# Filter samples loaded early, filter stores and first ffn loads by GpSimd, branch matrices one in two steps, the first image's lags kept for the tail

## The chip, the core and the metric

The kernel runs on one core of one Trainium2 chip, as a single launch. A core has a matrix engine (TensorE, PE in the profile, with its weight loads as PEld), VectorE (DVE), ScalarE (ACT), GpSimd (POOL) and SyncE (SP). Each engine works through its own queue in order. Transfers (DMA) are issued from the queues of SP, ACT and POOL, and an issue that waits for a semaphore holds up what stands behind it in its queue. The metric is the device time of the launch in microseconds (us), the median of several executions.

## What is computed

The input is two images of 128 channels and 64 x 64 places, all in 32-bit floats. Layer 0 is a neighbourhood-attention block. Layer 1 takes the 4096 places of an image as tokens: a full attention of normalised tokens with themselves, then a "spectral" ffn: causal convolutions with 16 filters, mixed by four branches' matrices, and three short lags. Cut to what matters:

```python
# layer 0: group norm, then a neighbourhood-attention block on NHWC tokens
x = x + _L0_conv_ref(_gn(x), ...)          # 7x7 neighbourhood attention, 4 heads, three 128x128 products
# layer 1 on tokens t of shape (2, 4096, 128)
t = t + _L1_attn_ref(_ln_t(t))             # all 4096 tokens, own key left out
t = t + _L1_ffn_ref(_ln_t(t), ...)
...
def _L1_attn_ref(q):
    sim = jnp.einsum('blh,bmh->blm', q, q) * scale
    sim = jnp.where(diag[None, :, :], jnp.float32(-1000000000.0), sim)
    attn = jax.nn.softmax(sim, axis=-1)
    return jnp.einsum('blm,bmh->blh', attn, q)
...
def _compute_spectral(u, sigma, phi, Mpp, Mpm):
    U_plus, U_minus = _stu_conv(phi, u, PADDED_SL)     # causal convolutions with 16 filters
    s = sigma ** SIGMA_POW
    out = jnp.einsum('btkd,k,kde->bte', U_plus, s, Mpp)
    return out + jnp.einsum('btkd,k,kde->bte', U_minus, s, Mpm)
def _compute_ar_u(Mu, u):                              # three short lags
    for i in range(Mu.shape[0]):
        ui = jnp.pad(u, ((0, 0), (i, 0), (0, 0)))[:, :sl]
        out = out + jnp.einsum('btd,de->bte', ui, Mu[i])
...
for i, frac in enumerate((1, 2, 4, 8)):                # four branches, on the first T / frac tokens
    si = _stu(x[:, :T // frac], sigma, phi, M_u[i], M_phi_plus[i], M_phi_minus[i])
...
weights = y_hard - jax.lax.stop_gradient(y_soft) + y_soft   # softmax of log_weights + gumbel
return jnp.sum(stacked * weights, axis=-1)
```

## The kernel before, in words

**Stages.** Layer 0 comes first (0 to about 344 us), written out as an explicit plan of pieces. Then follow the full attention of image 0 (`attention(0, fill)`, about 344 to 762 us), the attention of image 1 (`attention(1, fill)`, about 762 to 1187 us), a short tail, and the convolution of the ffn in a transformed domain (from about 1235 us to the end). The tail and the convolution work on both images.

**The attention** goes over 36 pairs of 512-token chunks, four steps each. A step multiplies keys with queries (L927, L936), ACT makes exponentials (L932, L943), and PE multiplies them with the values (L985 for the chunk's own sum, L1057 for the other chunk's). As the matrix of weights is symmetric, its transpose serves the other chunk too: ACT stores the exponentials of four steps to memory (`sent`, tile eb, L959), SP loads them back in another layout (`moved`, tile et, L966, four loads), DVE finishes the transposition in blocks (`turned`, L975), and PE uses them some steps later. MOVE, TURN and DELAY give the numbers of steps between these.

**The filler.** After each step, `fill()` runs one piece of other work. First it lets `stores()` send one queued store, or two where more than three are queued. Then it asks the generators in `urgent`, then those in `steps`: a plain `yield` ends the fill, `yield True` passes the turn on to the next queue. Within most of the attention the order of all engines is that of the program, so the filler decides what stands where in each queue.

**What the filler carries.** In image 0: `drain` (what is left of layer 0), `branch_weights` (loads lw, gu and sg by SP; its pow of sg stands on POOL at L1252; then loads of m_u), `filters`, and `tokens(1)`. In image 1: what is left of image 0's chains, its lags, `for_ffn`. Urgent are the chains `after(b, c)`, one for each finished chunk: transposes to tokens (L1123), statistics on DVE (L183, L184) with a pow on POOL (L174), normalisation (L191), transposes back (L202), products with the transform tr (L1175, L1189), copies by ACT (tile uo, L1156), sums and differences (tile ub, L1160, on POOL during attention, on DVE in the tail), and stores to us. The stores go through a list: `fresh` enters one, `room()` sends old ones until at most three buffers' worth is waiting, as the tag "ub" has four buffers.

**`filters`** loads the filter samples by SP in four parts (tile pn, L1344, two buffers shared with the branch matrices), turns their order round on DVE (L1361), transforms them on PE (L1382), and adds up running sums on ACT and DVE (L1389, L1391). For each of 12 steps POOL makes sum and difference (fb, L1395), and in eight of them also their negative (fn, L1407). The 32 stores of these to gs are issued from ACT's queue.

**`short_lags(b, h)`** first copies the residual back (four steps), then makes four groups of three products with mu (L1221), added on DVE (L1237). There are two such generators for each image, so eight groups. In image 0 the groups are put into `steps` of the second attention, except one that the filler runs at the end of the first.

**`for_ffn`** waits until a piece of the first image's memory (`spare`) has been used and given back, takes the first image's memory over, and loads inv and, through `filter_matrices`, 32 parts of the branch matrices by POOL (tile st, L1299). They are added up on DVE with the branches' weights (L1321, L1323) and scaled on ACT (L1334), three loads ahead. At the end `load_blocks` loads the first four blocks of the convolution, each with four ct loads and one ut load, from SP's queue (L1484, L1492).

**The tail** runs the last chains of image 1 two at a time, with lag groups of image 1 between them. The memory of chains and stores is used again by the convolution's y, so the convolution's first copies (L1599) wait for the last stores.

Of the kernel before, what the change touches and what calls it, by code (L numbers as in the profile page):

```python
# [14 lines left out]
P = 128  # L15
# [6 lines left out]
KF = 16  # L22
# [80 lines left out]
def kernel(  # L103
# [773 lines left out]
    with ap_:  # L877
# [21 lines left out]
        zc = [tp.tile([P, 2, TH + 1], F32, name="zc"), tt0.rearrange("p (s t) -> p s t", s=2)]  # L899
        nc.gpsimd.memset(zc[0][:, :, 0:1], 0.0)  # L900

        def attention(b, fill):
# [183 lines left out]

        spare = [tok[0][:, 0:4, :]]
        adder = [nc.gpsimd]
# [26 lines left out]
        def after(b, c):  # L1115
# [20 lines left out]
            yield  # L1136
            borrowed = b == 1 and spare not in ([], [None])
            z = spare.pop() if borrowed else sp.tile([P, 4, P], F32, tag="z4", name="z4")
            stats = ln_statistics(kept_)
            yield True  # L1140
            yield True
# [55 lines left out]

            if borrowed:
                spare.append(None)

# [101 lines left out]
        def filter_matrices(mpl, mmi, pool):  # L1302

            parts_ = [(k0, dst, src, i) for k0 in range(0, KF, 4) for dst, src in ((mpl, m_plus), (mmi, m_minus)) for i in range(NBR)]
            to_come = iter(enumerate(parts_))
            loaded = []

            def load():
                for at, (k0, _, src, i) in to_come:
                    loaded.append(branch(src[:, k0 : k0 + 4], i, pool if at % 4 > 1 else None))  # L1310
                    return

            for _ in range(3):
                load()
                yield
            for k0, dst, src, i in parts_:
                load()
                st = loaded.pop(0)
                dst2 = dst[:, k0 : k0 + 4].rearrange("p k e -> p (k e)")
                if i == 0:  # L1320
                    nc.vector.tensor_scalar(dst2, st, wt[:, 0:1], None, ALU.mult)  # L1321
                else:
                    nc.vector.scalar_tensor_tensor(dst2, st, wt[:, i : i + 1], dst2, ALU.mult, ALU.add)  # L1323
                yield
                if dst is mpl or i + 1 < NBR:
                    continue
                a, d = (m[:, k0 : k0 + 4, :].rearrange("p k e -> p (k e)") for m in (mpl, mmi))
                s = sp.tile([P, 512], F32, tag="uo", name="mdiff", bufs=2)
                nc.vector.tensor_tensor(s, a, d, ALU.subtract)
                nc.vector.tensor_tensor(a, a, d, ALU.add)  # L1330
                for k in range(4):
                    ks = slice(k * P, (k + 1) * P)
                    for to, of in ((a, a), (d, s)):
                        nc.scalar.activation(  # L1334
                            to[:, ks], of[:, ks], AF.Identity, bias=0.0, scale=sg[:, k0 + k : k0 + k + 1]
                        )
                yield

        def filters():

            def lags(hh, e):

                pn = sp.tile([P, KF, 2, LG], F32, tag="st", name="pn")
                nc.sync.dma_start(  # L1344
                    out=pn.rearrange("p k l f -> p (k l) f"),
                    in_=bass.AP(
                        phi_pad.tensor, P - FB + (2 * P * hh + e) * FB, [[2 * FB, P], [PHW, 2 * KF], [1, LG]]
                    ),
                )
                return pn  # L1350

            ph = {}
            for hh in range(SG // 2):
                pns = [lags(hh, e) for e in range(2)]
                for _ in range(3):
                    yield
                for e, pn in enumerate(pns):
                    at = (2 * hh + e) * LL
                    ph[hh, e] = cm[1][:, at : at + LL].rearrange("p (l f k) -> p l f k", l=2, f=LG)
                    for l in range(2):  # L1360
                        nc.vector.tensor_copy(ph[hh, e][:, l], pn[:, :, l, ::-1].rearrange("p k f -> p f k"))  # L1361
            yield

            def store(src, r0, n, ri, s, i, o):
# [3 lines left out]
                )  # L1368
                fresh(to, src, nc.scalar)

            everything = [(r0, c0 + ri * P, (ri,), P) for r0, c0 in row_tiles for ri in range(2)]
            everything.append((left_row, left_col, (0, 1), 64))
            for r0, c0, parts_, m in everything:
                places = cm[1][:, SG * LL : (3 * SG) * LL].rearrange("p (j e c) -> p j e c", j=SG, e=2)
                for j in range(SG):
# [27 lines left out]
                    if 1 in parts_:  # L1403
                        mine = slice(m - n, m)
                        room()
                        fn = sp.tile([P, 2, LL], F32, tag="ub", name="fn", bufs=4)
                        nc.gpsimd.tensor_scalar(fn[mine], fb[mine], -1.0, None, ALU.mult)  # L1407
                        store(fn[mine], r0, n, 1, s, 1, 0)
                    yield

        def residual_of(lags):
# [3 lines left out]

        def filler(b, steps, kept=None):

            urgent, done = [], []
            crowd_[0] = urgent

            def fill(c=None):
# [10 lines left out]

                stores()
                for queue in (urgent, steps):
                    while queue:
# [36 lines left out]

        def blocks(q):


            ct = ctp.tile([P, 2, 2 * (FB + 2) * KF], F32, tag="ct", name="ct")
            for o in range(2):
                for l in range(2):
# [4 lines left out]
                    at = l * (FB + 1) * KF  # L1483
                    nc.sync.dma_start(out=ct[:, o, at : at + (FB + l) * KF], in_=src)  # L1484
            return ct

        first_blocks = []

        def inputs(b, q):

            ut = utp.tile([P, 2, P], F32, tag="ut", name="ut")
            nc.sync.dma_start(  # L1492
                out=ut,
# [4 lines left out]
        def load_blocks():  # L1498
            for q in range(4):
                ct = blocks(q)  # L1500
                yield
                first_blocks.append((ct, inputs(0, q)))
                yield
# [5 lines left out]
        def for_ffn():  # L1509

            nonlocal mpl, mmi, inv, mu1, ctp, utp
            while spare != [None]:
                yield True
            first_.close()
# [4 lines left out]
            inv = l1.tile([P, K2 // BC * 4 + 1, CQ], F32, name="inv")  # L1519
            ctp = ctx.enter_context(tc.tile_pool(name="blocks", bufs=5))  # L1520
            nc.gpsimd.tensor_copy(mu1, mu)
            nc.gpsimd.dma_start(out=inv, in_=nc.inline_tensor(t_out, "t_out").ap().rearrange("(a p) c -> p a c", p=P))
            with tc.tile_pool(name="mix", bufs=2) as mixp:
                yield from filter_matrices(mpl, mmi, mixp)
            utp = ctx.enter_context(tc.tile_pool(name="inputs", bufs=4))

# [4 lines left out]

        steps = [*left, *kept, for_lags(), for_ffn()]


        kept = []
        fill, left = filler(1, steps, kept)
        attention(1, fill)
        adder[:] = [nc.vector]
        crowd_[0] = [None, None]
        for gen in steps:  # L1540
            for _ in gen:
                pass
        *chains, residuals = left
        while chains:
            for gen in chains[:2]:
                if next(gen, 0) == 0:
                    chains.remove(gen)
                stores()
            next(kept[0], None)
        stores_left()  # L1550
        for _ in residuals:
            next(kept[0], None)
        for _ in kept[0]:
            pass
# [330 lines left out]
```

## Time and profile before

| what | value |
|---|---|
| three executions, us | 2010.49, 2010.69, 2013.98 (median 2010.69) |
| the profiled execution, us | 2008.28 |
| its span, us | 2006.6 |
| mean granted clock of PE | 0.984 |
| busy, us: PE, DVE, ACT, POOL | 1912.1, 943.3, 733.1, 728.1 |
| the chain that ended last, by engine | PE 78%, DVE 8%, POOL 6%, DMA 4%, issue 2%, ACT 1% |
| DMA queue of SP (q1) | 221,874 packets, 26.2% of 16 engines' span |
| DMA queue of ACT (q10) | 13,758 packets, 8.2% |
| DMA queue of POOL (q0) | 18,848 packets, 5.7% |
| et loads by SP | 216 of 256 KB |
| us stores by POOL | 64 of 256 KB (3.1 us to landing), 128 of 32 KB (3.9 us) |
| gs stores by ACT | 12 of fb and 4 of fn of 256 KB, 12 and 4 of 64 KB |
| branch matrices by POOL | 32 of 256 KB (5.8 and 5.9 us to landing) |
| filter samples by SP | 4 of 128 KB |

The profile is of one execution. Its slices divide the span in 40 equal parts, and each digit is a busy share in tenths. Rows by stretch give the start and end, the length, then for each engine the busy time and the number of instructions, the clock that PE was granted, and the DMA engines' busy share. Rows in order of time give the start, the length, the engine, the line, the operation, the tiles and a count. A bracket at the end is the time that the engine had stood idle before, and the engine and line that ended it. An engine name with q (SPq, ACTq) is the issue of a transfer from that engine's queue. Times are us unless marked ns.

### The profile page before, as it was taken

What the parts mean: (1) busy time and instruction counts of PE and PEld (TensorE: products, weight loads), DVE (VectorE), ACT (ScalarE), POOL (GpSimd) and SP (SyncE); (2) the same over time, 40 slices, a digit from 0 to 9 for tenths busy, and PEclk for the clock granted to TensorE, in tenths of its full rate; (3) what the DMA queues carried; (4) which work ended last, traced back from release to release, by engine and by line L of the source; (5) the groups of instructions that cost most, each with busy time, mean ns of one, the idle gap of its engine ahead of it and who ended that gap; (6) DMA issues with size and microseconds to landing.
All of it is one profiled execution on the core that took longest, in us unless ns stands there. A gap on an engine that the chain in (4) does not pass through costs nothing.

```text
span 2006.6 us, 50785 instructions
## 1 busy us (share of the span) xinstructions
PE 1912.1 (95%) x20504; PEld 1353.1 (67%) x20504; DVE 943.3 (47%) x2918; ACT 733.1 (37%) x1718; POOL 728.1 (36%) x1183
## 2 busy tenths in 40 slices
PE   6899998999899999999999997999999999999998
PEld 4577776444344444444444444999999999999987
DVE  5799996453454434343654355333333343333332
ACT  3788986322133233212323223222222222222221
POOL 4467887314432345404333344222222212222211
PEclk8999999999999999999999998999999999999999
DMA  5222221568575643838787623222222223222211
GB/s 155 62 62 61 61 60 41 174 163 234 167 201 160 171 121 106 244 91 251 230 222 192 168 68 84 69 66 67 67 68 56 54 73 87 66 68 66 68 39 44
DMA packets 254713, 226.20 MB, mean 113 GB/s; under 512 B 130543, under 2 KB 210431, under 8 KB 247056
## 3 DMA queue, kind: packets, MB, share of 16 engines
q1 hardware_dynamic: 221874, 126.86, 26.2%
q10 hardware_dynamic: 13758, 63.28, 8.2%
q0 software_dynamic: 18848, 32.82, 5.7%
q8 instruction: 163, 2.67, 0.6%
q14 instruction: 70, 0.57, 0.1%
HBM read 131.40 MB, written 91.25 MB: 111 GB/s over the span
## 4 chain that ended last, share of the span: by engine, by line
PE 78%; DVE 8%; POOL 6%; DMA 4%; issue 2%; ACT 1%; SPq 0%; DVEq 0%; ACTq 0%; POOLq 0%
PE acc L1613 28%; PE own L985 11%; PE bank L927 7%; PE pc L1594 7%; PE other L1057 6%; PE bank L349 2%; PE bank L559 2%; PE bank L202 2%; PE bank L936 2%; PE bank L1175 1%; DVE et L975 1%; POOL us L1093 1%; PE bank L1221 1%; DMA us<-ub 1%; PE bank L523 1%
## 5 line engine op out<-in xcount | busy, mean ns | idle before, releaser
L1599 DVE COPY y<-pc 128x512 f32<-128x512 f32 x320 | 206.2, 686 | 347.1 <-PE pc L1594 345.9
L1613 PE MATMUL acc<-y,mpl 32*128 32x256 f32 x5120 | 323.7, 380 | 0.8 <-DVE af L1623 0.8
L1613 PE MATMUL acc<-y,mmi 32*128 32x256 f32 x5120 | 315.8, 375 | 0.0
L1599 ACT COPY y<-pc 128x512 f32<-128x512 f32 x320 | 171.8, 589 | 393.8 <-PE pc L1594 380.7
L1613 PEld LDWEIGHTS acc<-y,mpl 32*128 32x128 f32 x5120 | 290.0, 186 | 7.2 <-DVE af L1623 1.3
L1613 PEld LDWEIGHTS acc<-y,mmi 32*128 32x128 f32 x5120 | 291.5, 185 | 2.9
L1624 POOL TENSOR_TENSOR af<-af 128x512 f32<-128x512 f32 x39 | 49.7, 1275 | 572.8 <-DVE af L1623 559.7
L932 ACT ACTIVATE e<-bank 128x512 f32<-128x512 f32 x216 | 129.2, 599 | 303.8 <-PE bank L927 278.1
L1057 PE MATMUL other<-e,tok 128*128 128x512 f32 x448 | 232.2, 600 | 5.6 <-DVE xa L1066 5.6
L985 PE MATMUL own<-et,tok 128*128 128x512 f32 x448 | 216.9, 607 | 19.0 <-DVE et L975 13.8
L927 PE MATMUL bank<-cm 128*128 128x512 f32 x432 | 224.5, 601 | 0.0
L1594 PE MATMUL pc<-ct,ut 32*128 32x256 f32 x2560 | 211.1, 377 | 2.8 <-DVE y L1599 2.8
L1594 PEld LDWEIGHTS pc<-ct,ut 32*128 32x128 f32 x2560 | 172.5, 186 | 8.8 <-DVE y L1599 4.9
L985 PEld LDWEIGHTS own<-et,tok 128*128 128x128 f32 x448 | 84.5, 193 | 131.0 <-issue 96.7
L1160 POOL TENSOR_TENSOR ub<-uo 128x256 f32<-128x256 f32 (+1 forms) x160 | 99.3, 654 | 195.6 <-ACT uo L1156 183.9
L975 DVE STREAM_TRANSPOSE et<-et 128x1024 f32<-128x1024 f32 x108 | 127.8, 1222 | 65.8 <-DMA et<-eb 63.7
L1057 PEld LDWEIGHTS other<-e,tok 128*128 128x128 f32 x448 | 82.0, 192 | 98.9 <-issue 83.6
L1093 POOL DMA_DIRECT2D us<-ub x192 | 130.4, 732 | 14.6 <-DVE ln_st L183 5.3
L927 PEld LDWEIGHTS bank<-cm 128*128 128x128 f32 x432 | 76.1, 191 | 74.1 <-issue 68.1
L546 ACT ACTIVATE p<-p,mn 128x196 f32<-128x196 f32 x256 | 114.4, 449 | 14.1 <-DVE mn L536 13.5
L174 POOL TENSOR_TENSOR ln_rs<-ln_rs,mhalf 128x4 f32<-128x4 f32 x24 | 25.2, 1051 | 216.9 <-DVE ln_rs L173 216.9
L1156 ACT COPY uo<-bank 128x512 f32<-128x512 f32 (+1 forms) x96 | 45.8, 517 | 102.4 <-PE bank L1175 69.2
(266 smaller groups left out, 2621.9 us busy)
## 6 DMA issues: line engine op xcount, KB each, us to landing
eb<-e ACTq DMA_DIRECT2D x54, 1024.0 KB
et<-eb SPq DMA_DIRECT2D x216, 256.0 KB
ut<-us SPq DMA_DIRECT2D x160, 128.0 KB
us<-ub POOLq DMA_DIRECT2D x64, 256.0 KB, 3.1
ct<-gs SPq DMA_DIRECT2D x320, 40.0 KB
vw<-vd SPq DMA_DIRECT2D x256, 49.0 KB
ct<-gs SPq DMA_DIRECT2D x320, 32.0 KB
vd<-v SPq DMA_DIRECT2D x128, 32.0 KB
```

The source lines that it names most:

```text
L546: nc.scalar.activation(p, p, AF.Exp, bias=t[name + "mn"][:, h : h + 1], scale=-1.0, accum_out=t["den"][:, u, h : h + 1],)
L927: nc.tensor.matmul(ps.rearrange("p (q t j) -> p q t j", q=4, t=4), lhsT=cm[b][:, n * P : (n + 1) * P], rhs=keys.rearrange("p (t q j) -> p ...
L932: nc.scalar.activation(e, ps.rearrange("p (q r) -> p q r", q=4), AF.Exp, bias=0.0, scale=ASCALE)
L975: in_place(nc.vector.transpose(flat, flat))
L985: nc.tensor.matmul(out_, lhsT=tok[b][:, n, :], rhs=e, start=first, stop=last, skip_group_check=True)
L1057: nc.tensor.matmul(turn(other, "p (q r) -> p q r"), lhsT=tok[b][:, n, :], rhs=es[j], start=(j == 0), stop=(j == 3),)
L1093: by.dma_start(out=to, in_=part)
L1160: adder[0].tensor_tensor(ub[:, sgn, 0:n], both[:, 0:n], both[:, n : 2 * n], op)
L1594: nc.tensor.matmul(pcs[j].rearrange("p (g o c) -> p o g c", g=4, o=2)[:, :, at], lhsT=ut[rows_, par, :], rhs=cv_[rows_], start=True, stop= ...
L1599: (nc.scalar.copy if j % 2 else nc.vector.tensor_copy)(y[:, :, :, 4 * kl + j, :], pcs[j].rearrange("p (g x k) -> p k g x", g=4, k=KF))
L1613: nc.tensor.matmul(acc[j][:, 0:256], lhsT=(mmi if l else mpl)[rows_, k, :], rhs=y[rows_, k, 2 * l : 2 * l + 2].rearrange("p s n x -> p (s ...
L1624: eng.tensor_tensor(af[:, 0:2], af[:, 0:2], af[:, 2:4], ALU.add)
```

## The change

- The four loads of filter samples are issued by SP as soon as the attention's memory is there, into zc, a tile that nobody uses until the first chain writes it; `filters` no longer loads or waits for buffers.
- The stores to gs are issued by POOL, as those to us already are. The negative fn is made on DVE straight from the running sums, in two halves; before, POOL made it from fb. After each of its steps `filters` passes one turn on, so it runs in every second fill where nothing is urgent.
- `for_ffn` leaves `steps` and becomes `slow`: one step in every second fill, beside the other work, from the start of the second attention. The wait for `spare` and the borrowing go away. Five loads are ahead for three, and the extra pool has four buffers for two.
- The first four blocks of the convolution (16 ct and 4 ut loads) are issued by POOL. Later ones stay on SP.
- The lag groups of image 0 that are left after the first attention are kept (`held`) and run in the tail, one in each round.

```diff
@@ in the attention's set-up
+        pns = {}
+        for hh in range(SG // 2):
+            for e in range(2):
+                at = 1 + (2 * hh + e) * 2 * LG * KF
+                pns[hh, e] = zc[0][:, 0, at : at + 2 * LG * KF].rearrange("p (k l f) -> p k l f", k=KF, l=2)
+                nc.sync.dma_start(
+                    out=pns[hh, e].rearrange("p k l f -> p (k l) f"),
+                    in_=bass.AP(
+                        phi_pad.tensor, P - FB + (2 * P * hh + e) * FB, [[2 * FB, P], [PHW, 2 * KF], [1, LG]]
+                    ),
+                )
...
@@ filter_matrices
-                    loaded.append(branch(src[:, k0 : k0 + 4], i, pool if at % 4 > 1 else None))
+                    loaded.append(branch(src[:, k0 : k0 + 4], i, pool if at % 6 > 1 else None))
...
-            for _ in range(3):
+            for _ in range(5):
@@ filters
-            for hh in range(SG // 2):
-                pns = [lags(hh, e) for e in range(2)]
-                for _ in range(3):
+            for (hh, e), pn in pns.items():
+                at = (2 * hh + e) * LL
+                ph[hh, e] = cm[1][:, at : at + LL].rearrange("p (l f k) -> p l f k", l=2, f=LG)
+                for l in range(2):
+                    nc.vector.tensor_copy(ph[hh, e][:, l], pn[:, :, l, ::-1].rearrange("p k f -> p f k"))
+                if e:
                     yield
...
-                fresh(to, src, nc.scalar)
+                fresh(to, src)
...
-                        nc.gpsimd.tensor_scalar(fn[mine], fb[mine], -1.0, None, ALU.mult)
+                        one, two = sums[mine, 0, :], sums[mine, 1, :]
+                        nc.vector.scalar_tensor_tensor(fn[mine, 0, :], one, -1.0, two, ALU.mult, ALU.subtract)
+                        nc.vector.tensor_tensor(fn[mine, 1, :], two, one, ALU.subtract)
                         store(fn[mine], r0, n, 1, s, 1, 0)
                     yield
+                    yield True
@@ filler
+                if turns_[0] % 2:
+                    next(slow, None)
@@ blocks, inputs, load_blocks
-                ct = blocks(q)
+                ct = blocks(q, nc.gpsimd)
                 yield
-                first_blocks.append((ct, inputs(0, q)))
+                first_blocks.append((ct, inputs(0, q, nc.gpsimd)))
@@ for_ffn
-            while spare != [None]:
-                yield True
...
-            with tc.tile_pool(name="mix", bufs=2) as mixp:
+            with tc.tile_pool(name="mix", bufs=4) as mixp:
@@ second attention and tail
-        steps = [*left, *kept, for_lags(), for_ffn()]
+        steps, held = [*left, for_lags()], kept
+        slow = for_ffn()
...
+        held = [step for gen in held for step in (gen,) * 4]
+        held = (next(gen, None) for gen in held)
         while chains:
             for gen in chains[:2]:
                 if next(gen, 0) == 0:
                     chains.remove(gen)
                 stores()
             next(kept[0], None)
+            next(held, None)
```

## The prediction

> **What bounds the kernel now.** I read the page's slices first, then the busy times by stretch, then the order of time around each place where TensorE (PE) stands still.
>
> ```profile
> PE   6899998999899999999999997999999999999998
> ...
> core 0: us, PE busy (x) PEld busy (x) DVE busy (x) ACT busy (x) POOL busy (x), PEclk, DMA share, GB/s
> 430.00:475.00 45.00, 40.39 (x110) 18.00 (x109) 20.60 (x47) 10.59 (x19) 4.74 (x7) 0.96 0.73 164
> ...
> 500.00:535.00 35.00, 25.00 (x78) 11.14 (x78) 13.15 (x28) 4.87 (x11) 24.67 (x27) 0.95 0.67 192
> ...
> 1000.00:1030.00 30.00, 25.90 (x64) 12.04 (x63) 13.98 (x23) 8.07 (x21) 15.90 (x23) 0.94 0.90 237
> ...
> 1095.00:1120.00 25.00, 20.42 (x57) 8.56 (x56) 8.27 (x25) 6.52 (x11) 3.82 (x5) 0.93 0.72 195
> ...
> 1186.00:1238.00 52.00, 41.94 (x202) 22.63 (x202) 30.72 (x118) 15.15 (x27) 30.23 (x44) 0.90 0.28 82
> ```
>
> PE is busy 95% of the span. From 1243 us on (the convolution) it hardly pauses, and nothing of the change lies there. What can be won is the pauses between 344 and 1243 us. Each costs twice: the idle time, and a lower clock behind it (PEclk below 1.00). Idle plus (1 - clock) x length, by row: 430:475 6.4 us, 500:535 11.8, 1000:1030 5.9, 1095:1120 6.3, 1186:1238 15.3. The order of time says whose each pause is:
>
> ```profile
> 440.15 10.98 SPq L1344 DMA_DIRECT2D pn<-in_phi_pad_dram  x3
> ...
> 465.51 3.49 PE L985 MATMUL own<-et,tok 128*128 128x512 f32 x4 [3.66 <-DVE et L975]
> ...
> 510.14 0.52 ACTq L1093 DMA_DIRECT2D gs<-fn  x1
> 510.70 0.60 ACT L932 ACTIVATE e<-bank 128x512 f32<-128x512 f32 x1 [10.36 <-POOL fn L1407]
> 511.35 1.12 PE L936 MATMUL bank<-cm 128*128 128x512 f32 x2 [1.88 <-ACT e L932]
> ...
> 1017.19 0.49 DVE L1321 TENSOR_SCALAR mmi<-st,wt 128x512 f32<-128x512 f32 x1 [5.99 <-DMA st<-in_m_minus_dram]
> ...
> 1018.46 0.47 PE L949 MATMUL bank<-ident,e 128*128 128x128 f32 x1 [3.51 <-ACT e L943]
> ...
> 1110.12 3.66 PE L985 MATMUL own<-et,tok 128*128 128x512 f32 x4 [4.20 <-DVE et L975]
> ...
> 1208.33 0.49 PE L202 MATMUL bank<-ident,z 128*128 128x128 f32 x2 [3.88 <-DVE z L191]
> ```
>
> The reader is to see, in brackets, the idle time and who ended it: a block on the SP queue, stores on ScalarE's (ACT) queue that make the exponentials wait, VectorE (DVE) waiting for a branch matrix, SP again, and a chain that is too thin in the tail.
>
> **Part 1, filter samples early.** Out: the four pn loads in SP's queue at 434 to 451 us. The third and fourth wait there for a buffer, and the et loads behind them go out at 451.2. Gain: the pause before 465.51 with its half-speed matmuls, about 5.5 of the row's 6.4 us.
> In: the same four loads go out at about 340.6 us, behind tr and **ahead of sg** on SP. Sg is waited for in GpSimd's (POOL) queue:
>
> ```profile
> 340.60 0.50 SPq L1248 DMA_DIRECT2D sg<-in_sigma_dram  x1
> ...
> 348.48 2.93 POOL L1252 TENSOR_TENSOR sg<-sg,quarter 128x16 f32<-128x16 f32 x1
> ...
> 354.55 3.12 POOL L720 TENSOR_SCALAR tok<-tt,kmv,krs 128x128 f32<-128x128 f32 x4
> ...
> 357.73 0.33 PE L202 MATMUL bank<-ident,tok 128*128 128x128 f32 x1 [0.45 <-POOL tok L720]
> ```
>
> A pn load is 128x32 pieces of 32 bytes. The trace's packet records show 4096 such packets in a burst of about 2.2 us, four times 8.8. Sg landed about 4 us after its issue, behind tr, near 345. Behind four pn it lands near 354.5, and POOL's pow starts there instead of at 348.5: 6 us late. Queued behind it are the m_u loads, krs and tok, and PE waits for tok now already (357.73), so the delay reaches PE whole, with some 1.5 us of lower clock as after the pause at 465. **Loss 7.5 us**. Ends: 0, if the samples don't hold sg up; 11, if each load takes 3 us.
>
> **Part 2, filter stores and fn.** Out of ACT's queue: 32 gs stores (12+12 of fb, 4+4 of fn). They wait there for POOL's fb and fn, and exponentials queue behind: the 11.8 us of 500:535. Off POOL: 8 fn of about 1.49 us, 11.9 us. Onto DVE: 16 halves; the nearest row, DVE's 128x256 add on L1160, is 449 ns, so 7.2 us; DVE is busy 13 of 35 us there, so it hides.
> Onto POOL: 32 issues. The us<-ub row gives 130.4 us for 192, 0.68 each: 21.8 us. A filter step now takes two fills instead of one. A fill is 418 us (344 to 762) over about 148 steps, 2.8 us; so 12 steps last some 68 us, and POOL has in them 12 x 1.41 us of fb, 21.8 of issues and about 17 of the us chain: 56 of 68. It fits, barely.
> The new wait: fn on DVE needs one of four ub buffers, free when a store has landed. Behind it on DVE stand the et transposes and the copies that free PSUM, for which PE waits. A store takes 0.68 plus 3.1 us to land; at the first fn pairs eight small us stores stand ahead. I put 3 us on it (ends 0 and 8 x 1 = 8). **Gain 11.8 - 3 = about 8.5 us.**
> Here a rule speaks against the change. The Trainium skill, page DMA: Bandwidth & Descriptors, section SWDGE vs HWDGE vs iDMA, sends plain transfers to SP or ACT, because GpSimd computes each descriptor in software; the page's specifications put its first byte at about 1 us against 0.6. By the rule 32 + 20 issues lose 0.4 us each, 21 us if all were waited for, and part 2 would be a loss. By the rows the issue itself is much alike (0.68 on POOL, 0.52 the unhindered gs<-fn on ACT), and the price of ACT's queue is the 10.36 us that its exponentials waited. I take the rows: nobody waits for a gs load until far later.
>
> **Part 3, branch matrices (slow).** Same 32 loads, 32 DVE updates and 32 ACT scalings, now from the start of the second attention in every second fill, with five loads ahead and six buffers for three and four. Five items at two fills of 2.8 us are over 20 us ahead; a load lands in 5.9 us. So DVE's waits go: 5.9 us (1000:1030), and I give 1.5 of the 3.4 us that PE idles between 905 and 1000. Gain 7.
>
> **Part 4, first ffn loads on POOL.** 16 ct and 4 ut leave SP, where the et loads of 1097.85 stood among them: up to 6.3 us. They cost POOL 20 x 0.68 = 13.6 us, spread over about 16 fills (45 us) in which it is about a third busy. The bytes stay the same and still share the DMA engines, so I take 4, and take off 1.5 for statistics (L174) waiting behind issues. Gain 2.5. Parts 3 and 4 together: **9.5 us**.
>
> **Part 5, lags for the tail.** Seven groups of three L1221 matmuls of the first image leave the second attention (862 to 898 us; the eighth ran at 764 and stays). The chain of waits has 2.58 us a group: **gain 18.1 us**, as PE is the bound there. They return in the tail before the last chain is through. There PE has 10.1 us idle and 5.2 us of lost clock. But the convolution's first copies wait for the last us stores to land (1237), and those follow the last chain's matmuls. Counting along PE: the first late transpose had 9.5 us between L1123 and L202; in the new order 16.2 us of matmuls stand there; after it two more groups, but no pauses at full clock. The last L1189 moves from 1223.8 to about 1229.4, +5.6. Both chains' 24 stores then come closer together on POOL (16.3 us of issues): some 2.4 more. DVE gets 24 x 0.28 + 8 x 0.2 = 8.3 us on top of 30.7 of 52, hidden. **Tail +8** (ends 3, where all 15.3 are filled, and 18, where none is).
>
> **Sum:** -5.5 + 7.5 - 8.5 - 9.5 - 18.1 + 8 = -26 us. Span 2006.6 - 26 = 1980.6. The profiled execution took 2008.28, 1.7 more than its span, and the median is 2010.69, another 2.4: 4.1 in all. **Forecast 1984.7, said as 1985 us.**
>
> **Rivals.**
> *The tail takes all of it back* (18 instead of 8): for it, the tail is a chain through DVE, POOL and stores, not PE alone; against, 15.3 us of slack. -16: 1994.7 us. Chance 0.20.
> *Everything hides*: the samples don't delay sg (0 for 7.5), and the tail pays 3. For it, SP's issue could slip between packets; against, sg already lands behind tr. -26 - 7.5 - 5 = -38.5: 1972 us. Chance 0.17.
> *GpSimd becomes the bound* (slower): its queue is in order, and 52 new issues stand ahead of statistics, adds and us stores. If all were on the path, 52 x 0.68 = 35 us: -26 + 35 = +9, 2020 us. It decides once more than three quarters of these issues are waited for. For it: 56 of 68 us in the filter stage, and the fn wait on DVE. Against: POOL idles most of 535 to 905 us. Chance 0.08.
> That the change doesn't do what it says: the built order shows the 32 stores, 20 loads and seven groups moved, so nothing for it.
>
> **Numbers.** Forecast 0.55, rivals 0.20, 0.17, 0.08. The range goes from just above the case where all hides, to beyond the tail rival with part of parts 2 and 3 lost: 1970 to 2001. A measurement tells about 0.2% (4 us) from no change. The slower case is partly within that: faster 0.90, same 0.03, slower 0.07.
>
> **What would show it.** sg's pow near 354 us and a PE pause of 5 to 7 us before tok's transposes (part 1); no ACT idle ended by POOL in the filter stage, but DVE idle ended by gs stores (part 2); no DVE idle ended by st loads (part 3); et no longer late beside ct (part 4); the second attention 25 to 28 us shorter and the tail 8 longer with PEclk near 1.00 (part 5). It is wrong if DVE stands at fn for over 10 us in sum, or if the tail grows by over 15.

## The result, and the profile after

The changed kernel takes **1997.75 us** (median of six runs, 1994.82 to 2002.71) where the kernel before, run beside it, takes 2010.24. The ratio is 0.994, with a 95% interval of 0.9923 to 0.9956. So it is faster by about 12.5 us; the forecast was 25.7. The sign was right and the time lies inside the range, but half of the gain is missing. The profiled execution has a span of 1997.2 us after 2006.6.

One edit of the change is missing from the list ahead of the prediction. In `after`, the chain now ends its fill after its statistics (a plain `yield` where a `yield True` passed the turn on). Every kernel below has it, so no run tells what it is worth.

To see where the gain went, I cut both profiled spans at four instructions that do not change: the first row of four weights matmuls of attention 0 (L936, now L947), the same row of attention 1, the last row of own<-e, and the convolution's first copy into y.

| stage, us | before | after | measured | forecast |
|---|---|---|---|---|
| attention 0 | 426.4 | 426.3 | -0.1 | -5.5 + 7.5 - 8.5 = -6.5 |
| attention 1 | 421.7 | 400.2 | -21.5 | -9.5 - 18.1 = -27.6 |
| tail | 45.1 | 54.9 | +9.8 | +8 |
| convolution to the end | 769.5 | 769.3 | -0.2 | 0 |

Layer 0, ahead of these, ended 2.5 us later with the same instructions. Over all runs below, the start of attention 0 lies between 343.9 and 348.1 us and the last stage between 766.2 and 770.2 us, though no edit touches either; that much of any span is not the change's. In the stages between, the four kernels with the same attention 0 (the changed one, e4, e5, e6) agree within 0.9 us there, which is why these stages are compared and not spans alone.

The busy shares of PE in 40 slices, and then the busy times by stretch of the changed kernel (busy us, count of instructions, granted clock PEclk, DMA share, GB/s):

```profile
PE   6899998899899999999999998999999999999998
```

```profile
core 0: us, PE busy (x) PEld busy (x) DVE busy (x) ACT busy (x) POOL busy (x), PEclk, DMA share, GB/s
344.00:430.00 86.00, 75.58 (x226) 36.95 (x225) 37.31 (x125) 26.02 (x50) 33.66 (x40) 0.94 0.65 152
430.00:475.00 45.00, 44.05 (x121) 20.22 (x120) 23.98 (x68) 10.12 (x18) 9.92 (x13) 1.00 0.64 182
475.00:560.00 85.00, 75.50 (x232) 33.67 (x231) 35.66 (x65) 19.04 (x35) 47.72 (x71) 0.94 0.70 207
765.00:862.00 97.00, 91.62 (x304) 42.34 (x303) 41.22 (x93) 32.87 (x63) 58.02 (x88) 0.96 0.72 208
...
1095.00:1170.00 75.00, 73.04 (x273) 35.99 (x272) 31.78 (x82) 21.28 (x41) 32.35 (x50) 1.00 0.42 120
1173.00:1228.00 55.00, 49.21 (x226) 24.42 (x224) 35.32 (x139) 13.79 (x26) 28.97 (x42) 1.00 0.26 76
```

The old holes are closed: 430:475 has the full clock and 1 us of pause, 1095:1170 the full clock and 2 us, and the tail (1173:1228) has the full clock, though still 5.8 us of pause. But there are new holes: 10.4 us of pause in 344:430 and 9.5 in 475:560, both at a clock of 0.94, and 5.4 in 765:862. The order of time names them:

```profile
343.13 10.56 SPq L906 DMA_DIRECT2D zc<-in_phi_pad_dram  x4
353.74 2.50 SPq L1255 DMA_DIRECT2D sg<-in_sigma_dram  x1
359.16 2.93 POOL L1259 TENSOR_TENSOR sg<-sg,quarter 128x16 f32<-128x16 f32 x1 [8.11 <-DMA sg<-in_sigma_dram]
365.22 3.13 POOL L720 TENSOR_SCALAR tok<-tt,kmv,krs 128x128 f32<-128x128 f32 x4
366.07 0.47 PE L202 MATMUL bank<-ident,tok 128*128 128x128 f32 x1 [7.64 <-POOL tok L720]
...
514.08 2.17 POOL L1103 DMA_DIRECT2D gs<-fb  x3
515.85 1.11 POOL L1103 DMA_DIRECT2D gs<-fn  x1
516.42 1.26 POOL L1103 DMA_DIRECT2D gs<-fb  x1
520.05 0.43 DVE L1401 SCALAR_TENSOR_TENSOR fn<-cm 128x256 f32<-128x256 f32 x1 [12.90 <-DMA gs<-fb]
520.40 0.42 DVE L1402 TENSOR_TENSOR fn<-cm 128x256 f32<-128x256 f32 x1
520.73 2.36 DVE L986 STREAM_TRANSPOSE et<-et 128x1024 f32<-128x1024 f32 x2
523.15 3.70 PE L996 MATMUL own<-et,tok 128*128 128x512 f32 x4 [9.00 <-DVE et L986]
...
792.83 11.33 SPq L977 DMA_DIRECT2D et<-eb  x8
805.53 2.37 DVE L986 STREAM_TRANSPOSE et<-et 128x1024 f32<-128x1024 f32 x2 [10.91 <-DMA et<-eb]
808.00 3.75 PE L996 MATMUL own<-et,tok 128*128 128x512 f32 x4 [4.94 <-DVE et L986]
```

Each of the three is read backwards. PE stands 7.64 us for tok on POOL; tok stands behind the pow of sg; sg stands in SP's queue behind four sample loads, which keep it for 10.56 us. PE stands 9.00 us for et on DVE; the transposition of et stands on DVE behind an fn that waited 12.90 us for a buffer, that is, for a store of fb which POOL had only just issued. And PE stands 4.94 us for an et that took 12.7 us from issue to use, among the first loads of the slow steps. The first two were to be tested first.

### The profile page after: what moved, and what is told of

It is laid out like the page before. It is cut to its first block, busy times and chain, and to the rows that moved or that the text cites. A ratio compares the mean times of both kernels' runs of the same rounds, so it can differ in the third digit from the quotient of the medians.

```text
span 1997.2 us, 50806 instructions
## 1 busy us (share of the span) xinstructions
PE 1906.4 (95%) x20504; PEld 1350.6 (68%) x20504; DVE 951.8 (48%) x2934; ACT 733.0 (37%) x1718; POOL 749.4 (38%) x1227
## 4 chain that ended last, share of the span: by engine, by line
PE 77%; DVE 8%; POOL 4%; DMA 4%; issue 2%; SPq 2%; ACT 1%; DVEq 0%; POOLq 0%; ACTq 0%
PE acc L1615 28%; PE own L996 12%; PE bank L938 7%; PE pc L1596 7%; PE other L1068 7%; PE bank L349 2%; PE bank L947 2%; PE bank L559 1%; PE bank L202 1%; PE bank L1184 1%; DVE et L986 1%; DMA et<-eb 1%; DMA us<-ub 1%; ACT p L546 1%; PE bank L1228 1%
## 5 line engine op out<-in xcount | busy, mean ns | idle before, releaser
L1601 ACT COPY y<-pc 128x512 f32<-128x512 f32 x320 | 171.9, 589 | 394.8 <-PE pc L1596 381.3
L1596 PEld LDWEIGHTS pc<-ct,ut 32*128 32x128 f32 x2560 | 172.9, 187 | 10.1 <-DVE y L1601 6.3
```

The lines of the kernel that those rows point to most:

```text
L1596: nc.tensor.matmul(pcs[j].rearrange("p (g o c) -> p o g c", g=4, o=2)[:, :, at], lhsT=ut[rows_, par, :], rhs=cv_[rows_], start=True, stop= ...
L1601: (nc.scalar.copy if j % 2 else nc.vector.tensor_copy)(y[:, :, :, 4 * kl + j, :], pcs[j].rearrange("p (g x k) -> p k g x", g=4, k=KF))
```

## The experiments

All comparisons are with the kernel before, run on the same chip. Stages are those of the table above, from each run's profiled execution.

| run | ratio (95% interval) | attention 0 | attention 1 | tail |
|---|---|---|---|---|
| the changed kernel | 0.9940 (0.9923 to 0.9956) | 426.3 | 400.2 | 54.9 |
| e1, sg ahead of the samples | 0.9874 (0.9851 to 0.9897) | 416.3 | 397.5 | 54.5 |
| e2, buffers of its own for fn | 0.9883 (0.9858 to 0.9908) | 417.5 | 396.6 | 54.4 |
| e3, both | 0.9849 (0.9828 to 0.9870) | 407.7 | 401.7 | 54.8 |
| e4, lags back in attention 1 | 0.9954 (0.9939 to 0.9970) | 426.1 | 419.0 | 44.7 |
| e5, ct and ut on SP | 0.9929 (0.9907 to 0.9952) | 426.6 | 400.5 | 55.2 |
| e6, matrices in the list of steps | 0.9905 (0.9888 to 0.9923) | 427.0 | 394.8 | 54.4 |
| e7, e3 with stores on ACT | 0.9817 (0.9800 to 0.9835) | 404.9 | 402.1 | 54.6 |
| e9, e7 with fn on POOL | 0.9804 (0.9784 to 0.9825) | 404.2 | 395.9 | 54.5 |
| e14, e9 with one fill a filter step | 0.9857 (0.9830 to 0.9884) | 414.0 | 400.1 | 54.8 |
| e11, e3 at one step in three | 0.9805 (0.9786 to 0.9824) | 407.6 | 394.6 | 54.8 |
| e10, e7 at one step in three | 0.9799 (0.9781 to 0.9817) | 405.0 | 396.0 | 54.7 |
| e13, e7 with a later start | 0.9807 (0.9781 to 0.9832) | 405.2 | 395.2 | 54.4 |
| e12, the least change | 0.9798 (0.9778 to 0.9817) | 405.2 | 395.2 | 54.0 |

### e1: sg ahead of the samples

```diff
         nc.gpsimd.memset(zc[0][:, :, 0:1], 0.0)
-        pns = {}
-        for hh in range(SG // 2):
...
         chosen = branch_weights()
         next(chosen)
+        pns = {}
+        for hh in range(SG // 2):
...
```

> The changed kernel with one move: the four loads of the filter samples are issued behind the loads of lw, gu and sg instead of ahead of them. Theory (sg late is what took part 1's gain): the four sample loads hold SyncE for 10.6 us, sg is issued at 353.7 and its pow on GpSimd runs near 359; without them ahead sg's pow runs near 350, the 8.5 us of TensorE idle before the transposes of tok (L202) go to about 1, and the stage from 344 to 430 loses about 2 us in place of 10 busy plus some of clock. About 9 us less than the changed kernel: ratio to the kernel before near 0.989 to 0.990 (about 1989 us) where the changed kernel has 0.9938. Rival (a later wait takes the place: the samples now come later and their copies on VectorE hold up the filters, or the tok of the first image is late for another reason): less than 3 us gained, 0.9925 or above, with the idle before L202 or a new one before L1375 in the profile.

Measured: 1987.76 us, attention 0 shorter by 10.0 us. The order of time of e1:

```profile
341.15 0.50 SPq L1244 DMA_DIRECT2D sg<-in_sigma_dram  x1
...
349.03 2.93 POOL L1248 TENSOR_TENSOR sg<-sg,quarter 128x16 f32<-128x16 f32 x1
...
356.28 0.27 PE L202 MATMUL bank<-ident,tok 128*128 128x128 f32 x1
```

(The step next(chosen) issues the loads of lw, gu and sg.) The pow is 10.1 us earlier, 8.1 when the 2.0 us are taken off by which e1's attention 0 starts earlier, and PE's transposes have no bracket, so no wait, at the first tok. The samples still keep SP for 10.17 us, behind sg now, and PE does not wait for them. The theory holds; the loss from the order on SP is 10 us.

### e2 and e3: buffers of its own for fn

```diff
-fn = sp.tile([P, 2, LL], F32, tag="ub", name="fn", bufs=4)
+fn = sp.tile([P, 2, LL], F32, tag="st", name="fn")         # two buffers, free in this stage
```

> The changed kernel with one edit: the tile fn takes the two buffers of the tag st (which the change has left free in this stage) instead of one of the four of the tag ub that fb and the parts for us share. Theory (VectorE at fn waits for an ub buffer whose store GpSimd has not issued yet, and the et copies behind it on VectorE make TensorE wait 9.0 us): VectorE's idle before fn goes from 12.9 to under 2, the 9.0 us wait of own<-et at 523 goes to under 2, and with the clock that the pause cost 8 to 12 us are saved: ratio near 0.989 (about 1987 to 1990 us). Rival (GpSimd's own queue of fb, ub and stores is what is late): the wait moves to fb or to the us parts on GpSimd and to whoever needs them, 0 to 3 us saved, 0.9925 or above.

Measured: 1988.3 us, attention 0 shorter by 8.8 us. Waits of DVE, first in the changed kernel, then in e2 (engine, line, what it waited for; us in total, times, longest):

```profile
DVE fn L1401 <- DMA gs<-fb: 12.9, 1, 12.9
DVE fn L1401 <- POOL fb L1388: 11.5, 1, 11.5
```

```profile
DVE fn L1401 <- DMA gs<-fn: 8.6, 3, 6.1
DVE fn L1401 <- ACT cm L1382: 7.5, 1, 7.5
```

DVE still waits at fn, and by more than the 2 us I expected, now for stores of fn itself and for ACT's part of the sums; but not with an et behind it that PE needs: the longest wait of own<-et for et is 5.3 us (the one at the start of attention 1) and not 9.0. The total of a wait says little; what stands behind it decides.

> Both edits of the two runs before in one kernel. If both theories hold, the gains add, since the two pauses are 150 us apart: 16 to 21 us less than the changed kernel, about 1977 to 1982 us, ratio 0.984 to 0.986. If the stage has slack of its own that one edit already uses (rival: the sum of the stage is set by VectorE or GpSimd work, not by these waits), the two together give hardly more than the better one alone.

Measured: 1982.18 us; attention 0 is 407.7, which is 18.6 us less, against 18.8 for the sum of 10.0 and 8.8. The gains add. But attention 1 does not keep e1's and e2's length, which the last group of runs takes up.

### e7, e9, e14: which edit cleared the filter stage

The forecast gave the 11.8 us lost in 500:535 before the change to the stores in ACT's queue. e7 puts them back there.

```diff
-                fresh(to, src)                 # POOL
+                fresh(to, src, nc.scalar)
```

> The kernel of e3 (samples behind sg, fn in buffers of its own) with the filter stores put back on ScalarE. Theory (the prediction's 8.5 to 11.8 us for taking the stores off ScalarE were right in kind, and it was only fn's wait that hid them): VectorE or TensorE wait again for stores that ScalarE issues, attention 0 becomes 6 to 12 us longer than e3's 407.7, about 1988 to 1994 us. Rival (fn's move to VectorE is what counts, the stores' queue does not): within 3 us of e3, 1979 to 1985 us.

Both of my readings fell: e7 is better than e3, by 2.8 us in attention 0 (404.9; e10 and e13, with the same attention 0, have 405.0 and 405.2, and e3 and e11 both have 407.7 and 407.6). So moving the 32 stores to POOL cost 2.8 us. The two lines of e3 that show it, a wait of PE and the waits of DVE for stores of fn (us in total, times, longest):

```profile
512.05 1.12 PE L1057 MATMUL other<-e,tok 128*128 128x512 f32 x2 [2.65 <-DVE xa L1066]
...
DVE fn L1390 <- DMA gs<-fn: 9.8, 3, 6.7
```

The longest of these waits, 6.65 us, ends at 510.63, and the xa that PE waits for stands right behind it on DVE. In e7 the longest wait of DVE for such a store is 2.6 us, and PE waits for no xa longer than 0.5 us. So the price is one of stores on POOL with fn on DVE; stores on POOL with fn on POOL were not run. e9 then also puts fn back on POOL.

```diff
-nc.vector.scalar_tensor_tensor(fn[mine, 0, :], one, -1.0, two, ALU.mult, ALU.subtract)
-nc.vector.tensor_tensor(fn[mine, 1, :], two, one, ALU.subtract)
+nc.gpsimd.tensor_scalar(fn[mine], fb[mine], -1.0, None, ALU.mult)
```

> The kernel of e7 (samples behind sg, fn in buffers of its own, filter stores on ScalarE) with fn computed by GpSimd again from fb, as before the change. It tells which half of part 2 took away the 11.8 us that TensorE lost from 500 to 535 in the kernel before, where ScalarE stood 10.4 us at stores of fn. Theory A (ScalarE stood at fn's stores because GpSimd computed fn late; VectorE's fn is what counts): the waits of TensorE for e of ScalarE come back near 505 to 535, attention 0 goes from 404.9 to 411 to 416 us, about 6 to 11 us slower than e7, 1983 to 1988 us. Theory B (with buffers of its own fn is early enough on either engine, and what cleared the stage is the buffers, or the samples' early copies): within 2 us of e7.

Attention 0 is 404.2: theory B. With both on the engines of the kernel before, 475:560 has no pause. What is left of the change in this stage is the buffers, the early samples, the chains' `yield`, and one line that makes a filter step take two fills:

```diff
                     yield
-                    yield True
```

> The kernel of e9 (samples behind sg, fn in buffers of its own, fn on GpSimd and stores on ScalarE as before the change) with one edit: a filter step again takes one fill, not two. e9 showed that with these the stage 475 to 560 has no pause at all (84.6 of 85 us), though fn and its stores are on the engines of the kernel before, which lost 10 us of 85 there. Theory A (it is the halved pace of the filter steps that cleared the stage: ScalarE's stores come half as often and GpSimd's fn is no longer late): the waits of TensorE for e of ScalarE come back, TensorE is busy under 80 of 85 us, attention 0 goes from 404.2 to 410 to 416 us, ratio 0.983 to 0.987. Theory B (the buffers of its own for fn, or the samples' early copies, cleared it): attention 0 stays within 2 us of 404.2, ratio 0.979 to 0.982.

The stretch 475:560 of e9, then of e14, and two lines of e14's order of time on ACT:

```profile
475.00:560.00 85.00, 84.62 (x273) 38.50 (x272) 33.16 (x68) 24.07 (x44) 47.64 (x61) 1.00 0.80 231
```

```profile
475.00:560.00 85.00, 78.25 (x243) 36.99 (x244) 36.27 (x96) 21.97 (x39) 40.77 (x52) 0.94 0.68 197
```

```profile
497.44 0.58 ACT L1371 COPY cm<-bank 64x512 f32<-64x512 f32 x1 [7.26 <-POOL fn L1389]
505.66 0.60 ACT L932 ACTIVATE e<-bank 128x512 f32<-128x512 f32 x1 [7.15 <-POOL fn L1389]
```

Theory A: the same wait as before the change, an exponential on ACT behind a store that waits for POOL's fn, comes back by that one line, and costs 9.8 us in attention 0. POOL and ACT are not too slow for the filters; the steps came too fast for them. (e14 is still 12.4 us better than the kernel before in this attention; what of that stays unexplained is said below.)

### e4: the lags

```diff
-        steps, held = [*left, for_lags()], kept
+        steps, held = [*left, *kept, for_lags()], []
```

> The changed kernel with part 5 undone: the remaining lag work of the first image goes back to the list of steps of the second attention and nothing of it is kept for the tail. Theory (part 5 is the larger share of what was won: 18.1 us out of the second attention, 8 to 10 back in the tail): attention 1 becomes 17 to 19 us longer (about 419), the tail about 9 to 10 shorter (about 45), so 8 to 9 us slower than the changed kernel, about 2006 us, ratio 0.9975 to 0.999. Rival (the tail pays what the attention saves; the gain of the second attention comes from the branch matrices at a slow pace and the transfers on GpSimd): within 3 us of the changed kernel, 0.993 to 0.9955.

Attention 1 is 18.7 us longer and the tail 10.2 shorter, as expected. The stages give the lags a net gain of 8.5 us. But the ratio, 0.9954, lies where the rival put it: it rose by only 0.0014 (2.8 us), and the two intervals overlap. So what the lags moved in each stage is shown, and their net gain in the median is not. (The profiled span of e4 was 7.3 us longer than the changed kernel's, with a last stage that happened to be 1.6 us shorter.)

### e5, e6, e11, e10, e13: the slow steps

```diff
-                ct = blocks(q, nc.gpsimd)              # e5; ut alike
+                ct = blocks(q)
```

> The changed kernel with part 4 undone: ct and ut are loaded by SyncE again, not by GpSimd. Theory (as the prediction had it: the 16 small loads in SyncE's queue stand ahead of et loads): an et wait of 2 to 3 us returns near 1000 us and the time is 2 to 3 us above the changed kernel, ratio 0.995 to 0.9955. Rival (at the slow pace the loads come where nothing is short, so the queue they use does not matter): within 1 us, ratio as the changed kernel's.

The rival holds: 400.5 against 400.2 us, no et wait near 1000. Part 4 is worth nothing here. e12 below has these loads on SP and not at the slow pace, and there too no wait of PE for et is over 1 us while they are issued (987 to 1053 us).

```diff
-                if turns_[0] % 2:                       # e6
-                    next(slow, None)
-        steps, held = [*left, for_lags()], kept
-        slow = for_ffn()
+        steps, held = [*left, for_lags(), for_ffn()], kept
```

> The changed kernel with the pace of part 3 undone: the branch matrices and first loads stand in the list of steps again, behind the after-work, one step at every turn that has nothing urgent; loads five ahead and four buffers stay as changed. Theory A (the prediction's: the slow pace is worth 7 us because VectorE no longer stands at a matrix that has not landed and the et wait at 1107 goes): attention 1 becomes 5 to 7 us longer, about 2003 to 2005 us. Theory B (the slow pace begins with the first turn of attention 1, so it gave away at once, by the 4.9 us wait for et at 808, most of what it won later; run e4 left 2.8 us for parts 3 and 4 together): within 3 us of the changed kernel, the wait at 808 gone or under 2 us and another of 4 to 6 us back after 900.

Theory B was right that the wait at 808 goes and that one comes after 900 (4.92 us at 942), but not in the size: attention 1 is 5.4 us *shorter* without the slow pace. The order of time of e6, to be set against the last three lines of the changed kernel's above:

```profile
793.54 11.50 SPq L977 DMA_DIRECT2D et<-eb  x8
803.58 2.37 DVE L986 STREAM_TRANSPOSE et<-et 128x1024 f32<-128x1024 f32 x2 [7.63 <-DMA et<-eb]
...
806.06 1.96 PE L996 MATMUL own<-et,tok 128*128 128x512 f32 x4 [1.01 <-POOL ub L1169]
...
942.16 3.48 PE L996 MATMUL own<-et,tok 128*128 128x512 f32 x4 [4.92 <-DVE et L986]
```

From issue to use et takes 10.0 us here and 12.7 us there, where GpSimd issues inv at 772 and six parts of the matrices between 782 and 801 us; in e6 these first loads come at 860 us.

```diff
-                if turns_[0] % 2:
+                if turns_[0] % 3 == 0:                  # e11, e10
```

> The kernel of e3 with one edit: the branch matrices, the scaling of inv and the first loads advance at every third turn of attention 1, not at every second. In e3 they are done at 1020 us, 190 us before the conv begins, so there is room. Theory (the et waits of 4.9 us at 790 and 3.9 us at 928 come from the matrices' loads beside et): one or both shrink, 3 to 8 us less than e3, about 1974 to 1979 us. Rival (the wait at 790 comes from the us stores and eb of the turn from attention 0 to 1, the other moves with the pace): within 2 us of e3.

> The kernel of e7 with the pace of e11 (every third turn). If both act in their own stages (stores on ScalarE 2.8 us in attention 0, the pace 7 us in attention 1), they add: attention 0 near 405, attention 1 near 395, about 1968 to 1971 us, ratio 0.978 to 0.980. If the gain of e7 was of the same kind (fewer DMA issues on GpSimd), less than half of one of them adds: 1972 to 1976 us.

```diff
-            slow = iter(slow)                           # e13
+            slow, begin = iter(slow), turns_[0] + 20
-                if turns_[0] % 2:
+                if turns_[0] > begin and turns_[0] % 2:
```

> The kernel of e7 with one edit: the slow steps begin 20 turns (about 50 us) after attention 1 has begun and keep the pace of every second turn, so they end near 1075 us. Theory (the et wait of 4.7 us at 786 comes from inv and the first matrices loaded beside the last us stores and et of the turn between the attentions; the run with the steps behind the after-work did not have it): that wait goes to under 1 us, with the clock 5 to 7 us less than e7 in attention 1, unless the wait at 924 grows: about 1969 to 1972 us. Rival (any 256 KB load beside et costs the same, now or later): the wait moves to about 50 us later or adds to the one at 924, within 2 us of e7 (1976.7).

The wait at the start of attention 1 in e7, then in e13:

```profile
786.03 3.65 PE L985 MATMUL own<-et,tok 128*128 128x512 f32 x4 [4.74 <-DVE et L975]
```

```profile
785.33 1.96 PE L985 MATMUL own<-et,tok 128*128 128x512 f32 x4 [1.69 <-POOL ub L1158]
```

All three shorten attention 1, by different waits. At one step in three (e11 after e3, e10 after e7) the wait near 925 goes, from 3.9 and 4.9 us to none over 1.4, and the one near 790 stays (4.9 and 4.4). With the later start (e13) the one near 785 goes from 4.7 to 1.7 us, now for POOL's ub, and the one near 920 falls from 4.9 to 2.8. e10 did not reach the time I gave it, 1973.53 us and not 1968 to 1971: its attentions are as expected (405.0, 396.0), but its last stage is 770.2 us, where e11 has 766.2.

At every second step from the first turn, attention 1 took 400.2, 397.5, 396.6, 401.7, 400.5, 402.1, 395.9 and 400.1 us in eight kernels, 399.3 in the mean. With one step in three, the late start, or the steps' list, it took 394.6 to 396.0 in five. So that pace costs about 4 us in the mean, between nothing (e9) and 7 us (e7 against e13) in a given kernel; what makes the wait near 925 be there or not (it is not in e9) stays open.

### e12: the least change

Kept are the early samples (behind sg), two fills a filter step, five matrices ahead in six buffers, fn's own buffers, and the lags in the tail. Both moves of part 2, the slow pace and part 4 are undone. (The chains' `yield` and the missing wait for `spare` stay too.)

> Of the change only these are kept: samples early (behind sg), five branch matrices ahead in six buffers, two fills to a filter step, lags of the first image in the tail; fn has buffers of its own. Undone are both moves of part 2, the slow pace of part 3 and part 4. Theory (what the moves of stores, fn, ct and ut to other engines and the slow pace brought is nothing or less): attention 0 near 404 us, attention 1 near 395 us (as in e6), tail near 55, together about 1968 to 1973 us, ratio 0.978 to 0.981. Rival (the edits need each other: with the matrices behind the after-work and ct, ut on SyncE the loads fall beside et again): attention 1 over 399 us, 1975 us and above.

Measured: 1971.84 us, ratio 0.9798, interval 0.9778 to 0.9817. It is faster than the kernel before by 2% and than the changed one by about 1.4%. e9, e10, e11 and e13 lie within its interval, so which of the five is best was not told apart; e12 is the one with the fewest moves.

## Why the prediction was half right

By stage the forecast was -26.1 us and the profiles show -12.0: 6.4 us are missing in attention 0, 6.1 in attention 1, 1.8 in the tail. Two steps failed, part 2 in attention 0 and parts 3 and 4 in attention 1, and one term of part 1 was too small.

**Part 1, out: right.** The pause before the et at 465 is gone; 430:475 has clock 1.00. What it brought by itself was not run.

**Part 1, in: right in mechanism, too small.** I put 6 us of delay and 1.5 of clock on sg, 7.5. It was 10.0 (e1). The failed term is "behind four pn it lands near 354.5", which sets four packet bursts of 2.2 us one behind the other and lets sg be issued at once. But a load of this kind holds the queue for what stands behind it. The four issues in the changed kernel, then in the kernel before (ns, shortest, median and longest):

```profile
L906 SPq DMA_DIRECT2D zc<-in_phi_pad_dram x4: 501/2974/3986, 343.1 to 351.6; - x4
```

```profile
L1344 SPq DMA_DIRECT2D pn<-in_phi_pad_dram x4: 368/396/2074, 434.9 to 449.1; - x4
```

The first issue takes 0.5 us, those right behind another 2.1 to 4.0. So sg was only *issued* at 353.7, and its pow started at 359.2: 8.1 us late, with the later start of the stage taken off, and not 6. The kernel before showed it already, in the 2.07 us of the one pn that stood right behind another. The upper end, 11, came from 3 us a load; it was near.

**Part 2: the first step that failed.** "The 11.8 us of 500:535" was given to the stores' engine, and "Gain 11.8 - 3 = about 8.5". The runs show four terms. The two fills a step, which I had used only to count the time POOL has, bring 9.8 us (e9, e14). The stores on POOL cost 2.8 (e3, e7). fn on DVE in a shared buffer costs 8.8, and not 3 (e2); 8 was my upper end. fn's engine in itself is within 1 us (e7, e9). That sums to 9.8 - 2.8 - 8.8 = -1.8 where 8.5 were forecast. The sum starts from e14, whose fn has buffers of its own; what these bring to an fn on POOL, as in the kernel before, was not run. The sentence "wrong if DVE stands at fn for over 10 us in sum" came true, with 24.4; but 11.5 of it, before 505.20, made PE wait nowhere over 0.8 us.

**Attention 0 does not close.** With part 1's 5.5 out and 10.0 in and these 1.8, it would be 6.3 us longer; it is 0.1 shorter. So 6.4 us were gained that neither the prediction nor a run of mine accounts for. The kernel before had one more pause that the prediction does not list:

```profile
625.51 2.02 PE L1057 MATMUL other<-e,tok 128*128 128x512 f32 x2 [2.17 <-DVE xa L1066]
```

The clock in 615:640 is 0.93 there. In the changed kernel, e9 and e14 no wait of PE between 560 and 700 us is over 1 us. Ahead of that xa on DVE stand the statistics of a chain and of the tokens, run in one fill, which fits the edit of the chains' `yield`; but that edit was not run alone, and the cause stays open. So the misses in this stage were larger (2.5 us in part 1, 10.3 in part 2) than the 6.4 us missing in the table.

**The rule that was weighed.** The Trainium skill, page DMA: Bandwidth & Descriptors, section SWDGE vs HWDGE vs iDMA, sends plain transfers to SP or ACT. I took the rows against it. For the stores the rule had the right sign, at 2.8 us for 32 issues, or 0.09 each, far from the 0.4 that the prediction estimated from the first bytes in the page's Specifications; for ct and ut the queue made no difference (e5). The 10.36 us on which I set it aside were not the price of ACT's queue, but of the pace (e9, e14).

**Part 3: the second step that failed.** Parts 3 and 4 together were to bring 9.5 us; attention 1 less the lags' 18.7 shows 2.8. I gave 7 us for VectorE's waits at the matrices. These waits are gone, and with the steps in their list again (e6) attention 1 is 394.8 us, which is 8.2 less than the 403.0 that 421.7 less the lags' 18.7 leaves. So the deeper look-ahead and what goes with it (more buffers, no wait for `spare`, the chains' `yield`; not told apart) had that size; the slow pace took 5.4 of it back. The failed step is the pace taken as free: I had looked for late matrices and not for what their earlier loads do to et.

**Part 4: part of that step.** 2.5 us forecast, nothing measured (e5). The pause at 1110 was put down to ct and ut in SP's queue; it is gone with them still there (e5, e12).

**Part 5 and the tail: right, in the stages.** 18.1 forecast, 18.7 measured by e4; tail 8 forecast, 9.8 to 10.2 measured, at clock 1.00 as said. The rival in which the tail takes all 18 back gave 1994.7 us, near the measured time, but by a wrong cause: the tail took 10.

**The measure of a hole.** I priced pauses as idle time plus (1 - clock) x length. For 344:430 this gives 10.4 + 0.06 x 86 = 15.6 us against 2.0 in e1, a difference of 13.6, where e1 saved 10.0; for e14's 500:535 it gives 6.8 + 5.3 = 12.0, where e9 saved 9.8. It overstates by 36 and 22%. Over all of attention 0, with the same matmuls, PE in e1 is idle for 7.5 us less than in the changed kernel and busy for 2.5 us less, while (1 - clock) x length falls by 5.1; from e14 to e9 the three are 5.5, 4.4 and 5.1. So the clock term is larger than the time by which the matmuls were longer, in the first pair by half. A likely reason, not tested, is that the clock recorded during the pause itself is low too, and so the pause is partly counted twice.

## What to carry to other kernels

In this kernel a load put early in a queue was paid for by what stands behind it: look for the small load that is needed soon behind a block of loads of many small pieces, and put it ahead. When an operation changes its engine, ask which buffers its output shares and what stands behind it on the new engine; a wait is as dear as the first thing behind it that the bound engine needs. Where work is fed in between other work, test the pace first: here one line of pace did what moving stores and arithmetic between engines was thought to do, and a feed that starts with the first turn loads its inputs just when the buffers of the stage before are moving.

## What the hardware showed unexpectedly

SP's queue took a load of 4096 pieces of 32 bytes in 0.4 to 0.5 us when no such load stood right ahead of it, but 2.1 to 4.0 us when one did: four in a row kept it for 10.56 us, and 10.17 in e1. Even the small sg load took 2.50 us to issue behind them, and 0.50 ahead of them in e1. And sg's value was not usable until 5.4 us after its issue began (353.74 to 359.16).
